# Decoder layer with 32 experts: the product of gate and up stays in SBUF on its way to the down product

## The chip, the cores and the metric

The kernel runs on one core of a Trainium2 chip. The core has a matrix engine (PE, with a separate stream for weight loads, PEld), a vector engine (DVE), a scalar engine (ACT), a general engine (POOL) and an engine that mostly issues transfers (SP). SP, ACT and POOL each have a queue from which they start transfers; all transfers run on the same 16 DMA engines. Every engine works through its own list in order and waits for others by semaphores. Matrix products accumulate in PSUM, everything else lies in SBUF (128 partitions) or in device memory (HBM).

The metric is the device time of the launch in microseconds. Before the change it was 3912.97 us, the median of three runs from 3909.75 to 3914.64.

## What is computed

One decoder layer in float32 on 32 sequences of 128 tokens of width 512: causal self-attention, cross-attention, and a mixture of experts with a shared expert. The change is in the experts. Each of 4096 tokens picks 6 of 32 experts; cut to what matters:

```python
g = ragged_dot(xs, w_gate, group_sizes)      # xs: tokens sorted by expert, width 512 -> 352
u = ragged_dot(xs, w_up, group_sizes)
d = ragged_dot(silu(g) * u, w_down, group_sizes)   # 352 -> 512
expert_out = sum over the 6 picks of d * weight
out = x + expert_out + shared(x)
```

## The kernel before

Self-attention and cross-attention fill the first half of the time. While cross-attention ends, tokens are routed: tables in memory say which token stands in which slot of which expert. The slots are cut into 208 tiles of 128 tokens, each of one expert. Four sets of weight buffers (`SETS`) are used in turn, and consecutive tiles belong to four different experts, so a set keeps its expert for several tiles; a register (`fresh`) says whether a weight transfer really has to be made, and a transfer that need not be made is skipped (`cond=new`).

`Experts.run` (from L1508) writes the order of PE, DVE, ACT and POOL out by hand. Iteration i does:

- `gate_up(i)`: PE multiplies the turned tokens `e_xT` with `wg` and `wu` (16 matmul records of 352 columns, L1447) into the two halves of a PSUM tile; ACT makes silu of the first half (`e_act`, L1451); DVE multiplies it with the second half (`e_gu`, L1452). `e_gu` is one buffer of 128 slots x 384 columns, of which 352 are written and the rest is zero. A transfer of ACT's queue writes it to memory (`e_gu_d`, L1454), cut into 4 runs of 96 columns.
- `turn_in(i + 2)`: DVE transposes gathered tokens in 32x32 blocks (`e_xr` to `e_xT`, L1434).
- `turn_out(i - 1)`: DVE transposes `e_gr` to `e_guT` in two instructions, 96 and 32 partitions (L1473).
- `weights_in(i + 4)`: SP's queue loads `wg` and `wu` (L1396) for the tile four on.
- `down(i - 2)`: PE multiplies `e_guT` with `wd` (6 matmul records of 512 columns, L1483); ACT scales by the routing weight (`e_y`, L1487); POOL's queue adds the rows into `sum_d` in memory (indirect, L1488). `weights_out(i + 2)` loads `wd` in two parts (L1408, L1411).
- `part_out(i)`: a second transfer of ACT's queue reads `e_gu_d` back as `e_gr` (L1463), so that partition 32q + s holds run q of the slots 4s to 4s + 3. It can be issued when the first has landed.
- `tokens(i + 5)`: four indirect gathers of POOL's queue (`e_xr`, L1422).

So the product of tile i has one iteration to become `e_gr`, and the transpose of it one more until PE needs it. PSUM has four tiles, taken in turn by `gate_up` and `down`. `e_y` and `e_gr` have two buffers each.

Before and after the experts stand groups of the shared expert (`Shared.group`, L1201 to L1262): three before, five after. Their work space (`s_p`), and that of cross-attention (`x_p2`), stay allocated during the experts. After `experts.run()` a conditional block handles more than 208 tiles; it is not entered here. The last groups end the kernel.

Of the kernel before, what the change touches and what calls it, by code (L numbers as in the profile page):

```python
# [10 lines left out]
F32 = mybir.dt.float32  # L11
# [7 lines left out]
P = 128  # L19
E = 512  # L20
# [1244 lines left out]
class Experts:  # L1265
# [14 lines left out]
    def __init__(  # L1280
        self, cm, ctx, table_ds, h3_d, sum_d, w_gate, w_up, w_down, eid, fresh, rows, n_tiles
    ):
        self.cm, self.h3_d, self.sum_d, self.eid, self.fresh = cm, h3_d, sum_d, eid, fresh
        self.w_in, self.w_out, self.n_tiles = (w_gate, w_up), w_down, n_tiles
        nc, tc = cm.nc, cm.tc

        def pool(name, bufs):
            return ctx.enter_context(
                tc.tile_pool(name=name, bufs=bufs, side="right", reuse_waits="tile")
            )  # L1290

        cp, self.p2 = pool("e_c", 1), pool("e_p2", 2)
        self.dram = ctx.enter_context(tc.tile_pool(name="e_dram", bufs=4, space=DRAM))
        T = h3_d.shape[0]
        self.T, self.cp, self.rows, self.table_ds = T, cp, rows, table_ds
        self.NT = rows.shape[1]
        self.wg = [cp.tile([P, EC, M], F32, name=f"wg{s}") for s in range(SETS)]
        self.wu = [cp.tile([P, EC, M], F32, name=f"wu{s}") for s in range(SETS)]
        self.wd = [cp.tile([P, len(M_CHUNKS), E], F32, name=f"wd{s}") for s in range(SETS)]

        self.gu_s = cp.tile([P, self.Q * self.RUN], F32, name="e_gu")

        self.row_i = cp.tile([P, 2], I32, name="e_row_i")
        self.row = cp.tile([P, 2], F32, name="e_row")
        self.last, self.expert = None, {}
        self.got, self.spread = {}, {}
        self.xr, self.xT, self.gu, self.gr, self.guT = {}, {}, {}, {}, {}

    def fetch(self):

        nc = self.cm.nc
        for j in range(self.NT):
            self.got[j] = [
                self.p2.tile([P, E], F32, name=("e_y", "e_xT")[j % 2])[:, 0 : 2 * P].rearrange(
                    "p (s o) -> p s o", o=2
                )
                for i in range(len(self.table_ds))
            ]
            for t, table_d in zip(self.got[j], self.table_ds):
                nc.gpsimd.indirect_dma_start(  # L1320
                    out=t.rearrange("p s o -> p (s o)"),
                    out_offset=None,
                    in_=table_d.rearrange("(n s) o -> n (s o)", s=P),
                    in_offset=bass.IndirectOffsetOnAxis(ap=self.rows[:, j : j + 1], axis=0),
                    bounds_check=table_d.shape[0] // P - 1,
                )
        nc.gpsimd.memset(self.gu_s, 0.0)
        nc.gpsimd.iota(self.row_i, pattern=[[0, 2]], base=self.T + 1, channel_multiplier=1)

    def arrange(self, j):  # L1330
# [108 lines left out]
    def gate_up(self, i):  # L1439
        if i >= self.end:  # L1440
            return
        nc = self.cm.nc
        pgu = self.cm.banks()
        t, s = self.xT.pop(i), i % SETS
        for half, w in enumerate((self.wg[s], self.wu[s])):
            for c in range(EC):
                nc.tensor.matmul(  # L1447
                    pgu[:, half, 0:M], t[:, c, :], w[:, c, :], start=c == 0, stop=c == EC - 1
                )
        act = self.p2.tile([P, M], F32, name="e_act", bufs=1)  # L1450
        nc.scalar.activation(act, pgu[:, 0, 0:M], AF.Silu)  # L1451
        nc.vector.tensor_tensor(self.gu_s[:, 0:M], act, pgu[:, 1, 0:M], ALU.mult)  # L1452
        self.gu[i] = self.dram.tile([self.Q, P, self.RUN], F32, name="e_gu_d")
        nc.scalar.dma_start(  # L1454
            out=self.gu[i].rearrange("q s m -> s q m"),
            in_=self.gu_s.rearrange("s (q m) -> s q m", q=self.Q),
        )

    def part_out(self, i):


        gr = self.gr[i] = self.p2.tile([P, self.Q, self.RUN], F32, name="e_gr")
        self.cm.nc.scalar.dma_start(  # L1463
            out=gr.rearrange("p t m -> p (t m)"),
            in_=self.gu.pop(i).rearrange("q (i t) m -> (q i) (t m)", t=self.Q),
        )

    def turn_out(self, i):
        g = self.gr.pop(i)
# [8 lines left out]
    def down(self, i):  # L1478
        nc = self.cm.nc
        py = self.cm.banks()[:, 0, :]  # L1480
        t, s = self.guT.pop(i), i % SETS
        for c, (_, n) in enumerate(M_CHUNKS):
            nc.tensor.matmul(  # L1483
                py, t[:n, c, :], self.wd[s][:n, c, :], start=c == 0, stop=c == len(M_CHUNKS) - 1
            )
        y = self.p2.tile([P, E], F32, name="e_y")
        nc.scalar.mul(y, py, self.weight[:, i : i + 1])  # L1487
        nc.gpsimd.indirect_dma_start(  # L1488
            out=self.sum_d[:, :],
            out_offset=bass.IndirectOffsetOnAxis(ap=self.into[:, i : i + 1], axis=0),  # L1490
            in_=y[:, :],
            in_offset=None,
            bounds_check=self.T + P - 1,
            compute_op=ALU.add,
        )
# [12 lines left out]
    def run(self):  # L1508


        first, en = self.first, mybir.EngineType
        with self.cm.tc.manual_schedule(engines={en.PE, en.DVE, en.Activation, en.Pool}):
            for i in range(first, first + 2):
                self.turn_in(i)
                self.tokens(i + 3)
            for i in range(first, self.end + 2):
                self.gate_up(i)
                self.turn_in(i + 2)
                if first < i <= self.end:
                    self.turn_out(i - 1)  # L1520
                self.weights_in(i + SETS)
                if i > first + 1:
                    self.down(i - 2)
                    self.weights_out(i - 2 + SETS)
                if i < self.end:
                    self.part_out(i)
                self.tokens(i + 5)


# [1 line left out]
def decoder_kernel(  # L1531
# [31 lines left out]
    with tc.tile_pool(name="x_w", bufs=1, side="right") as x_w:  # L1563
# [29 lines left out]
        s_w = SharedWeights(cm, s_w_pool, sw_gate, sw_up, sw_down)  # L1593
        s_h_pool = ctx.enter_context(tc.tile_pool(name="s_h", bufs=2, reuse_waits="tile"))
        shared = Shared(cm, s_h_pool, h3T_d, sum_d, out)
        p2 = ctx.enter_context(tc.tile_pool(name="x_p2", bufs=2, reuse_waits="tile"))
        cross.run(p2)
        x_ctx.close()
        s_pool = ctx.enter_context(tc.tile_pool(name="s_p", bufs=1, reuse_waits="tile"))
        shared.use(s_pool, s_w)  # L1600
        en = mybir.EngineType
        in_order = {en.PE, en.DVE, en.Activation, en.Pool}
# [19 lines left out]
    with tc.manual_schedule(engines=in_order):  # L1622
# [16 lines left out]
        shared.group(EARLY - 1, False, between)  # L1639
        while todo:  # L1640
            between()
    experts.run()
    many = nc.values_load(used[0:1, 0:1], min_val=1, max_val=n_tiles)
    with tc.If(many > usual):
        experts.begin(usual, n_tiles)
        experts.first_tokens()
        experts.run()
    done = EARLY * Shared.G
    for i in range(2):
        b = done // 2  # L1650
# [59 lines left out]
```

## Time and profile before

| | us |
|---|---|
| median of 3 runs | 3912.97 |
| profiled execution, device time | 3913.15 |
| its span, first to last instruction | 3911.4 |
| experts, first gate matmul to first matmul of the next shared group | 2024.05 to 3618.70 |
| PE busy in 2400 to 2800 us | 388.15 of 400 |
| DVE, ACT, POOL busy there | 135.89, 60.35, 299.81 |
| mean share of the 16 DMA engines there | 0.69 |
| issue of `e_gu_d`, of `e_gr` on ACT's queue | 0.366, 0.338 |

The profile is of one execution. A page gives busy times, slices and costly groups; a row of a group reads: line, engine, operation, out<-in, shapes, count, then busy time and mean ns of one, then the idle time of the engine just before such instructions and what ended most of it. A row of the timeline reads: start, duration, engine, line, operation, out<-in, shapes, count, and in brackets the engine's idle time before it with its releaser. A row of the waits reads: who waited for whom, total us, times, longest. "issue" and "remote" mean that the profile does not name a releaser. Matmul ends are modelled and overlap the next start a little.

### The profile page before, as it was taken

What the parts mean: (1) busy time and instruction counts of PE and PEld (TensorE: products, weight loads), DVE (VectorE), ACT (ScalarE), POOL (GpSimd) and SP (SyncE); (2) the same over time, 40 slices, a digit from 0 to 9 for tenths busy, and PEclk for the clock granted to TensorE, in tenths of its full rate; (3) what the DMA queues carried; (4) which work ended last, traced back from release to release, by engine and by line L of the source; (5) the groups of instructions that cost most, each with busy time, mean ns of one, the idle gap of its engine ahead of it and who ended that gap; (6) DMA issues with size and microseconds to landing.
All of it is one profiled execution on the core that took longest, in us unless ns stands there. A gap on an engine that the chain in (4) does not pass through costs nothing. (4 is left out here: it accounts for less than half of the span.)

```text
span 3911.4 us, 58185 instructions
## 1 busy us (share of the span) xinstructions
PE 3793.0 (97%) x19060; PEld 2015.6 (52%) x19060; DVE 2057.6 (53%) x3202; ACT 1678.9 (43%) x4032; POOL 2349.5 (60%) x2582
## 2 busy tenths in 40 slices
PE   8999999899999999999999999999999999999999
PEld 5666666434444444444445555555555555555444
DVE  5888888777877877776133333333333333332111
ACT  6989999757766776666101111111111111111000
POOL 3545545636777777775347777777777777775000
PEclk9999999899999999999999999999999999999999
DMA  3111110121111111111167777767667676766210
GB/s 110 34 34 38 37 34 27 43 87 57 53 60 47 47 47 47 49 47 50 52 178 168 164 166 170 174 151 174 160 153 167 161 170 147 181 151 150 80 64 32
DMA packets 285987, 387.21 MB, mean 99 GB/s; under 512 B 147888, under 2 KB 179248, under 8 KB 285616
## 3 DMA queue, kind: packets, MB, share of 16 engines
q0 software_dynamic: 62912, 109.85, 15.7%
q1 hardware_dynamic: 81792, 190.98, 15.4%
q10 hardware_dynamic: 140976, 82.60, 7.5%
q8 instruction: 154, 2.52, 0.3%
q14 instruction: 153, 1.25, 0.1%
HBM read 617.52 MB, written 143.07 MB: 194 GB/s over the span
## 5 line engine op out<-in xcount | busy, mean ns | idle before, releaser
L1422 POOL DMA_INDIRECT e_xr<-h_d,e_run_of x832 | 849.2, 1021 | 282.1 <-issue 268.1
L695 DVE TENSOR_REDUCE nm<-ps 128x2 f32<-128x1024 f32 x512 | 611.2, 1216 | 112.1 <-PE ps L691 105.3
L1452 DVE TENSOR_TENSOR e_gu<-e_act,ps 128x352 f32<-128x352 f32 x208 | 108.4, 521 | 974.4 <-ACT e_act L1451 548.8
L718 ACT ACTIVATE xp<-ps 128x1024 f32<-128x1024 f32 x512 | 505.9, 1021 | 265.0 <-PE ps L691 200.9
L1483 PE MATMUL ps<-wd,e_guT 128*128 128x512 f32 (+1 forms) x1248 | 585.2, 605 | 34.6 <-ACT e_y L1487 15.7
L714 PE MATMUL ps<-xqn,xk 32*128 32x512 f32 x2048 | 527.1, 620 | 20.6 <-ACT xp L718 19.2
L1447 PE MATMUL ps<-wu,e_xT 128*128 128x352 f32 x1664 | 528.6, 461 | 7.4 <-DMA wu<-in_L_ffn_w_up_dram 5.1
L1447 PE MATMUL ps<-wg,e_xT 128*128 128x352 f32 x1664 | 527.9, 460 | 5.3 <-DMA wg<-in_L_ffn_w_gate_dram 4.5
L691 PE MATMUL ps<-xk,xq 32*128 32x512 f32 x2048 | 526.9, 630 | 0.5 <-DVE nm L695 0.4
L1451 ACT ACTIVATE e_act<-ps 128x352 f32<-128x352 f32 x208 | 96.5, 464 | 935.2 <-PE ps L1447 443.7
L1488 POOL DMA_INDIRECT sum_d<-e_y,e_into x208 | 335.8, 1615 | 178.1 <-ACT e_y L1487 91.6
L1447 PEld LDWEIGHTS ps<-wg,e_xT 128*128 128x128 f32 x1664 | 315.1, 190 | 243.2 <-issue 108.8
L1447 PEld LDWEIGHTS ps<-wu,e_xT 128*128 128x128 f32 x1664 | 316.4, 191 | 186.6 <-DMA wu<-in_L_ffn_w_up_dram 8.3
L279 ACT ACTIVATE s<-s,a_nm 128x128 f32<-128x128 f32 x1024 | 395.7, 396 | 4.9 <-DVE a_nm L265 4.5
L1483 PEld LDWEIGHTS ps<-wd,e_guT 128*128 128x128 f32 (+1 forms) x1248 | 239.8, 194 | 291.7 <-issue 226.5
L1487 ACT ACTIVATE e_y<-ps,e_weight 128x512 f32<-128x512 f32 x208 | 143.0, 687 | 431.3 <-PE ps L1483 265.0
L714 PEld LDWEIGHTS ps<-xqn,xk 32*128 32x128 f32 x2048 | 168.6, 183 | 284.3 <-ACT xp L718 123.3
L1473 DVE STREAM_TRANSPOSE e_guT<-e_gr 96x384 f32<-96x384 f32 (+1 forms) x416 | 230.5, 554 | 76.2 <-DMA e_gr<-e_gu_d 53.5
L228 POOL TENSOR_SCALAR k<-kz,a_keep,a_extra 128x256 f32<-128x256 f32 x128 | 82.6, 655 | 287.4 <-ACT kz L227 287.4
L1028 POOL DMA_INDIRECT table_d<-entry,at x192 | 202.1, 1053 | 64.7 <-issue 53.2
L729 PE MATMUL ps<-xp,v 128*32 128x512 f32 x2048 | 233.0, 595 | 7.9 <-ACT xp L718 7.6
L1434 DVE STREAM_TRANSPOSE e_xT<-e_xr 128x512 f32<-128x512 f32 x208 | 226.3, 1088 | 8.8 <-DMA e_xr<-h_d,e_run_of 8.8
(272 smaller groups left out, 5282.6 us busy)
## 6 DMA issues: line engine op xcount, KB each, us to landing
wg<-in_L_ffn_w_gate_dram SPq DMA_DIRECT2D x208, 704.0 KB
wu<-in_L_ffn_w_up_dram SPq DMA_DIRECT2D x208, 704.0 KB
wd<-in_L_ffn_w_down_dram SPq DMA_DIRECT2D x208, 576.0 KB
e_gu_d<-e_gu ACTq DMA_DIRECT2D x208, 192.0 KB
e_gr<-e_gu_d ACTq DMA_DIRECT2D x208, 192.0 KB
wd<-in_L_ffn_w_down_dram SPq DMA_DIRECT2D x208, 128.0 KB
e_xr<-h_d,e_run_of POOLq DMA_INDIRECT x832
xres<-in_x_dram SPq DMA_DIRECT2D x32, 256.0 KB
```

What stands on the lines that cost most here:

```text
L279: nc.scalar.activation(s[:, j, c, side, :], s[:, j, c, side, :], AF.Exp, bias=nm[n][:, side, at : at + 1], accum_out=sm[n][:, to : to + 1],)
L691: self.nc.tensor.matmul(sc[:, i, :], q[rows, ts(c, P)], k[rows, :], start=True, stop=True)
L695: self.nc.vector.tensor_reduce(at[:, self.ROW[side], 2 * pair : 2 * pair + 2], sc, AX.X, ALU.max, negate=True)
L714: self.nc.tensor.matmul(sc[:, i, :], k[rows, ts(c, P)], q[rows, :], start=True, stop=True)
L718: self.nc.scalar.activation(e, sc, AF.Exp)
L729: self.nc.tensor.matmul(po[b, side][ts(j, 32), :], self.v2[b % 2][:, c, 2 * j + side, :], es[j // 2][:, j % 2, :], start=c == 0, stop=c == ...
L1422: self.cm.nc.gpsimd.indirect_dma_start(out=xr[:, t, :], out_offset=None, in_=self.h3_d.rearrange("t (q f) -> (t q) f", q=self.Q), in_offse ...
L1434: self.cm.nc.vector.transpose(xT.rearrange("p c (t i) -> p c t i", t=self.Q), self.xr.pop(i).rearrange("p t (j c) -> p c t j", c=EC),)
L1447: nc.tensor.matmul(pgu[:, half, 0:M], t[:, c, :], w[:, c, :], start=c == 0, stop=c == EC - 1)
L1473: self.cm.nc.vector.transpose(t[rows, 0:n, :].rearrange("p c (t i) -> p c t i", t=self.Q), g[rows, :, 0 : 32 * n].rearrange("p t (j c) -> ...
L1483: nc.tensor.matmul(py, t[:n, c, :], self.wd[s][:n, c, :], start=c == 0, stop=c == len(M_CHUNKS) - 1)
L1488: nc.gpsimd.indirect_dma_start(out=self.sum_d[:, :], out_offset=bass.IndirectOffsetOnAxis(ap=self.into[:, i : i + 1], axis=0), in_=y[:, :] ...
```

## The change

The memory tile `e_gu_d` and `part_out` go. After the multiplication, four transfers of ACT's queue each copy one run of 96 columns from all 128 partitions of `e_gu` to 32 partitions of `e_gr`, within SBUF. `e_gu` has two buffers instead of one, `e_gr` three instead of two, and the scaled output (`e_y`, now `e_out`) four instead of two. They lie in a new pool, opened in the space of `x_p2` and `s_p`, which are closed before the experts; after them the new pool is closed and `s_p` is opened again for the last shared groups.

```diff
-        nc.vector.tensor_tensor(self.gu_s[:, 0:M], act, pgu[:, 1, 0:M], ALU.mult)
-        self.gu[i] = self.dram.tile([self.Q, P, self.RUN], F32, name="e_gu_d")
-        nc.scalar.dma_start(
-            out=self.gu[i].rearrange("q s m -> s q m"),
-            in_=self.gu_s.rearrange("s (q m) -> s q m", q=self.Q),
-        )
-
-    def part_out(self, i):
-        gr = self.gr[i] = self.p2.tile([P, self.Q, self.RUN], F32, name="e_gr")
-        self.cm.nc.scalar.dma_start(
-            out=gr.rearrange("p t m -> p (t m)"),
-            in_=self.gu.pop(i).rearrange("q (i t) m -> (q i) (t m)", t=self.Q),
-        )
+        gu = self.gu_s[i % 2]
+        nc.vector.tensor_tensor(gu[:, 0:M], act, pgu[:, 1, 0:M], ALU.mult)
+        gr = self.gr[i] = self.p3.tile([P, self.Q, self.RUN], F32, name="e_gr", bufs=3)
+        for q in range(self.Q):
+            nc.scalar.dma_start(
+                out=gr[ts(q, 32)], in_=gu[:, ts(q, self.RUN)]
+            )
+
+    def room(self, pool):
+        self.p3 = pool
+        self.gu_s = [pool.tile([P, self.Q * self.RUN], F32, name=f"e_gu{i}") for i in range(2)]
+        for t in self.gu_s:
+            self.cm.nc.gpsimd.memset(t, 0.0)
...
-        y = self.p2.tile([P, E], F32, name="e_y")
+        y = self.p3.tile([P, E], F32, name="e_out", bufs=4)
...
-                if i < self.end:
-                    self.part_out(i)
...
+    x_out.close()
+    e_out = ExitStack()
+    experts.room(e_out.enter_context(tc.tile_pool(name="e_p3", bufs=1, reuse_waits="tile")))
     experts.run()
...
+    e_out.close()
+    shared.use(ctx.enter_context(tc.tile_pool(name="s_p", bufs=1, reuse_waits="tile")), s_w)
```

## The prediction

> **What bounds the kernel.** I read the busy times first, then the groups of PE in the experts, then the waits, then the timeline of one tile that goes well and one that doesn't.
>
> ```profile
> PE 3793.0 (97%) x19060; PEld 2015.6 (52%) x19060; DVE 2057.6 (53%) x3202; ACT 1678.9 (43%) x4032; POOL 2349.5 (60%) x2582
> L1483 PE MATMUL ps<-wd,e_guT 128*128 128x512 f32 (+1 forms) x1248 | 585.2, 605 | 34.6 <-ACT e_y L1487 15.7
> L1447 PE MATMUL ps<-wu,e_xT 128*128 128x352 f32 x1664 | 528.6, 461 | 7.4 <-DMA wu<-in_L_ffn_w_up_dram 5.1
> L1447 PE MATMUL ps<-wg,e_xT 128*128 128x352 f32 x1664 | 527.9, 460 | 5.3 <-DMA wg<-in_L_ffn_w_gate_dram 4.5
> ```
>
> PE is busy 97% of the span. In the experts it stands still for 34.6 + 7.4 + 5.3 = 47.3 us, no more; the change can win only there, and in what such pauses bring with them.
>
> ```profile
> 3590.84 2.74 PE L1483 MATMUL ps<-wd,e_guT 128*128 128x512 f32 x6
> 3591.10 0.46 ACT L1451 ACTIVATE e_act<-ps 128x352 f32<-128x352 f32 x1 [4.11 <-PE ps L1447]
> 3592.15 0.37 ACTq L1454 DMA_DIRECT2D e_gu_d<-e_gu  x1
> 3593.42 2.53 PE L1447 MATMUL ps<-wg,e_xT 128*128 128x352 f32 x8
> 3593.62 0.69 ACT L1487 ACTIVATE e_y<-ps,e_weight 128x512 f32<-128x512 f32 x1 [2.05 <-PE ps L1483]
> 3594.33 0.34 ACTq L1463 DMA_DIRECT2D e_gr<-e_gu_d  x1
> 3598.15 2.31 PE L1483 MATMUL ps<-wd,e_guT 128*128 128x512 f32 x5
> ```
>
> This is a good tile: silu starts 0.26 us after PE turned to the down product, and the next down product follows 7.31 us after the last. The first gate matmuls start at 2024.05 in the first tile and 3600.73 in the last: 207 distances, 1576.7 us. At 7.31 they would take 1513.2, so 63.5 us are lost: 47.3 (2.0 of it behind the last tile) by pauses, about 16 by the slow clock after them (PEclk is 0.86 in 3278 to 3290 us and 0.80 in 3564 to 3578, each with one pause, against 1.00; such stretches last 3 us, once 7).
>
> ```profile
> 3188.41 2.74 PE L1483 MATMUL ps<-wd,e_guT 128*128 128x512 f32 x6
> 3195.81 0.46 ACT L1451 ACTIVATE e_act<-ps 128x352 f32<-128x352 f32 x1 [10.85 <-remote]
> 3196.31 0.52 DVE L1452 TENSOR_TENSOR e_gu<-e_act,ps 128x352 f32<-128x352 f32 x1 [10.49 <-ACT e_act L1451]
> 3196.75 1.07 DVE L1434 STREAM_TRANSPOSE e_xT<-e_xr 128x512 f32<-128x512 f32 x1
> 3197.74 1.10 DVE L1473 STREAM_TRANSPOSE e_guT<-e_gr 96x384 f32<-96x384 f32 x2
> 3198.95 4.14 PE L1483 MATMUL ps<-wd,e_guT 128*128 128x512 f32 x6 [3.06 <-ACT e_y L1487]
> ```
>
> A bad tile: silu comes 7.40 us after PE turned to the down product. DVE multiplies, turns the tokens, and only then turns the product that PE needs. PE pauses 3.06 us. So silu may be 7.40 - 3.06 = 4.34 us late, and every us more is a pause. The releaser that the row names is not the cause; the order on DVE is.
>
> ```profile
> PE ps L1483 <- ACT e_y L1487: 15.7, 7, 3.1
> PE ps L1483 <- issue: 6.6, 6, 2.0
> PE ps L1483 <- DVE e_guT L1473: 6.3, 2, 4.1
> PE ps L1483 <- DMA wd<-in_L_ffn_w_down_dram: 5.9, 3, 2.2
> q10 hardware_dynamic: 140976, 82.60, 7.5%
> ```
>
> Down products that pause without waiting for `wd`: 15.7 + 6.6 + 6.3 = 28.6, less the 2.0 at the very end: 26.6 us. Weights: 47.3 - 2.0 - 26.6 = 18.7. Going through the 26.6 in the timeline, ten pauses (1.35, 1.78, 1.06, 2.42, 2.53, 2.93, 3.06, 1.66, 2.23, 4.09: 23.1 us) follow an idle ACT with nothing in its own queue to explain it, as at 3195.81, where the row says "remote"; four (1.74, 0.49, 0.99, 0.30: 3.5 us) follow an ACT that was held until `e_gu_d` had landed. The last fence's queue, q10, is ACT's.
>
> **The change, part by part.** *The hold on ACT.* The second transfer waits on ACT's queue until the first has landed, with the next silu behind it: 2.18 us from issue to issue in the good tile (3592.15 to 3594.33), 4.60 at 2608.54 to 2613.14. Silu waits for it, DVE for silu, PE for DVE. This wait goes: -3.5 us, the four pauses; at least 0, if the unexplained idleness takes its place, and no more, as the ten are not of it.
>
> *Four issues for two.* An issue takes 0.366 and 0.338 us; four at most 4 x (0.37 + 0.04) = 1.64. They start 1.05 us after silu (3591.10 to 3592.15) and end at 2.69; the scaling of y, 2.52 us after silu now, starts 0.2 us later and ends at 3.4 of 7.31. Next late is POOL's scatter: per tile POOL needs 4 x (1.02 + 0.30) + 1.62 + 0.30 = 7.2 us. Behind it wait only gathers for tiles three on. Cost 0; without the 3.9 us that ACT has left, 0.94 us per tile, 196 in all. In the built program each transfer of SP's and ACT's queues takes one of eight semaphores in turn and waits until the last user has landed. Six per tile made ACT's wait for a weight transfer of SP now and then, and SP's for ACT's; eight per tile make each wait for its own counterpart one tile earlier, 7.31 us ago. Taken as 0.
>
> *The way of the data.* No row shows a copy within SBUF. From below: the store lands within 2.18 us, and the new transfer is one such hop. From above: four one after another, 8.7 us. The product of the tile issued at 2608.54 is turned at 2616.75: 8.2 us. At the upper end DVE is 0.5 us late, within the 4.34. I take the lower, as they are issued without waiting for each other: 0. The Trainium skill, page "DMA: Bandwidth & Descriptors", "Rules for kernel authors", speaks against this part: transfers to disjoint partition parts share the same 16 engines and serialize, so one transfer of 128 partitions is better. No run here shows it yet; by it the sum is the same, as even the serial case fits.
>
> *Less traffic.* The stage moves 163 GB/s over 1594 us, 260 MB; a round trip of 2 x 192 KB x 208 = 82 MB (82.60 in the row) becomes 41 MB, 16% of all bytes less. Packets: q10 has 140976 in 7.5% of 16 x 3911 us, 33 ns each. After it 208 x 512 = 106496 stay: 73 us less per DMA engine at 33 ns, 4.6 points of the stage's 0.69. At the far end, the gather queue's 156 ns (62912 packets in 15.7%), they would add 745 us per engine; packets of 384 bytes are nearest to q10's own. The idleness of the ten is unexplained, so its price is bounded: 0 if the traffic has no part in it, -23.1 if all. I scale lateness with the bytes: pause = 0.84 x (pause + 4.34) - 4.34, which gives 0.44, 0.80, 0.20, 1.34, 1.43, 1.77, 1.88, 0.70, 1.18, 2.74, together 12.5: -11. Weights: 1.44 MB take 5.0 to 8.6 us to arrive; 16% less is about 1.1 us at each of 13 pauses, at most -12; since a PE that pauses less also asks earlier, -5, from 0 to -12.
>
> *Clock.* Nine stretches at half speed, about 1.7 us each: those behind pauses over 1.9. Four of the ten fall under that, and the longest gets shorter: -8; 0 to -16.
>
> *Buffers and space.* More buffers of y remove 13.5 us of POOL and a little of ACT, neither on PE's path: 0. Two fills of 0.44 us on POOL instead of one are placed among the routing, beside idle stretches of 12.57 and 14.85 us: 0. At the end the reopened space waits for the last scatter (issued 3620.39, 1.55 us). Silu of the shared group stands at 3625.87, and PE can fill four PSUM tiles of 6.86 us first: 27 us of cover: 0; without it, about 3.
>
> Sum: -3.5 - 11 - 5 - 8 = -27.5 against the profiled execution's 3913.15 (its span is 3911.4, 1.75 lie around it, and it is within 0.2 of the median): **3886**.
>
> **Rivals.** *The late signals stay.* PE's pauses come from what the trace doesn't name, and weights hide what is left: -3.5 with 0 to -4 by weights: 3906 to 3913. For it: the ten pauses have no cause in ACT's queue. Against: ACT's longest idles all stand directly behind the transfer that reads memory.
>
> *More landings, more late silu.* The mechanism: ACT gets late behind its transfers' completions; a tile now completes 4 + 5 of ACT and POOL instead of 2 + 5. Place: silu, L1451; it decides beyond 4.34 us. Lateness x 9/7: 1.286 x (23.1 + 43.4) - 43.4 = 42.1, +19 us, and as much clock as 19/47 of 16, +6: 3938. For it: the idle stands behind transfer issues. Against: nothing is late for want of ACT's time, 60 us busy in 400.
>
> *All pauses go.* The experts at 7.31 per tile: 3913 - 63.5 = 3850; POOL's 7.2 is next. Against: weights arrive at the DMA's pace. That the transfers aren't four, or go through memory, is ruled out by the built program, which lists four to `e_gr` per tile.
>
> **How the numbers follow.** Forecast (3868 to 3905) 0.47; all or nearly all pauses gone (3848 to 3868) 0.12; late signals stay (3905 to 3921) 0.21; more late silu (above 3921) 0.20. A measurement of this kernel can tell about 0.2%, 7.8 us. Faster is the first two and a small part of the third, 0.60; same 0.20; slower 0.20. The range from 3855 to 3922 leaves out most of the slow rival and the end of the best case, together some 0.2.
>
> **What would show it.** After: no row of `e_gu_d`; q10 with about 107,000 packets and 41 MB; L1483's idle near 15 to 18 us and not 34.6; L1447's together near 8; silu never held behind its queue. Right in mechanism if the down products pause less and silu is less often late; wrong if L1483's idle stays at 30 or grows, or if DVE waits for `e_gr`. A different stage's time would show a cost that I placed at 0.

## The result, and the profile after

The changed kernel was slower. It took 3944.98 us (median of 4 runs, 3941.12 to 3951.21) against 3911.36 (4 runs, 3909.07 to 3914.64) of the kernel before; the ratio is 1.0087, 95% interval 1.0069 to 1.0104. The forecast was 3886, range 3855 to 3922.

The busy times, the queue of ACT and the groups of PE in the experts, from the page of the changed kernel (span 3944.9 us):

```profile
PE 3798.7 (96%) x19060; PEld 2016.3 (51%) x19060; DVE 2052.9 (52%) x3202; ACT 1674.5 (42%) x4032; POOL 2349.6 (60%) x2583
q10 hardware_dynamic: 121008, 41.73, 4.3%
L1478 PE MATMUL ps<-wd,e_guT 128*128 128x512 f32 (+1 forms) x1248 | 592.5, 612 | 74.2 <-issue 73.8
L1443 PE MATMUL ps<-wg,e_xT 128*128 128x352 f32 x1664 | 527.2, 459 | 0.0
L1443 PE MATMUL ps<-wu,e_xT 128*128 128x352 f32 x1664 | 526.2, 459 | 0.0
```

The bytes went as planned (41.73 MB in ACT's queue, half of 82.60). The packets did not: ACT's queue has 121008 and not about 107,000, because each transfer also has 16 packets of 4 bytes (in the experts 208 x (512 + 4 x 16) = 119808), which the prediction left out. PE no longer stands still for gate and up weights at all (7.4 + 5.3 us before). But the pauses ahead of the down product grew from 34.6 to 74.2 us: +27 us of pauses in all. The distances between the first gate products of the 208 tiles now lose 98.9 us against 7.31 per tile, where it was 63.5. Of these 35 us more, 28 are pauses (73.5 instead of 45.3, without those behind the last tile) and the rest, 7, is the slow clock that follows them (11 half-speed stretches instead of nine). The other stages did not move: the next shared group starts 33.5 us later, all of it gathered in the experts.

The timeline of the worst pause shows how it comes (start, duration, engine, line; in brackets the idle time before):

```profile
2548.43 2.81 PE L1478 MATMUL ps<-wd,e_guT 128*128 128x512 f32 x6
2551.08 2.53 PE L1443 MATMUL ps<-wg,e_xT 128*128 128x352 f32 x8
2553.45 2.53 PE L1443 MATMUL ps<-wu,e_xT 128*128 128x352 f32 x8
...
2559.63 0.07 SPq L1392 DMA_DIRECT2D wu<-in_L_ffn_w_up_dram  x1
2559.70 0.46 ACT L1447 ACTIVATE e_act<-ps 128x352 f32<-128x352 f32 x1 [8.00 <-remote]
2560.19 0.52 DVE L1449 TENSOR_TENSOR e_gu<-e_act,ps 128x352 f32<-128x352 f32 x1 [11.87 <-issue]
...
2560.63 1.08 DVE L1430 STREAM_TRANSPOSE e_xT<-e_xr 128x512 f32<-128x512 f32 x1
2560.75 2.52 ACTq L1452 DMA_DIRECT2D e_gr<-e_gu  x4
2561.62 1.11 DVE L1468 STREAM_TRANSPOSE e_guT<-e_gr 96x384 f32<-96x384 f32 x2
...
2562.84 3.36 PE L1478 MATMUL ps<-wd,e_guT 128*128 128x512 f32 x4 [6.86 <-issue]
```

The up product that silu (2559.70) reads had ended by 2548.31, just before PE turned to the down product; silu comes 11.4 us later, and ACT had nothing else to do for 8.00 of them. SP's `wu` transfer, which waits for the same signal of PE, starts at the same instant, 2559.63. So it isn't ACT that is late, but PE's signal: the semaphore records have it at 2559.61. Signals between ACT and DVE were prompt: in every tile the multiplication starts 0.03 us after silu's end or after DVE's instruction before it. PE meanwhile ran on to 2555.97 and then stopped for 6.86 us, since the product of the tile before stands behind silu's multiplication on DVE. The pause is the lateness less 4.5, as the prediction's threshold of 4.34 says. It is the bad tile of before; there are now more of them. Of the 40 pauses ahead of down products (without the end), 37, with 71.6 of 73.5 us, follow a silu that is over 4 us late. Silu starts over 0.3 us late in 116 tiles instead of 91, and 441 us late in sum instead of 230.

Where a wait is named can mislead here: the waits put 320 us of idle time ahead of the scaling of y down to the landing of `e_gr`, but the built program has that instruction wait only for PE and for an old scatter.

What changed for SP can be read in its waits (queue, line, what for: us in total, times, longest us), first of the kernel before, then of the changed one, both from 2100 to 3500 us:

```profile
SPq L1411 <- DMA wd<-in_L_ffn_w_down_dram: 188.5, 52, 9.6
SPq L1411 <- DMA e_gr<-e_gu_d: 69.6, 21, 6.2
```

```profile
SPq L1404 <- remote: 76.3, 29, 5.1
SPq L1392 <- PE ps L1443: 75.6, 61, 2.9
SPq L1404 <- PE ps L1478: 73.4, 42, 5.5
```

Before, SP waited for other transfers (the semaphore of the `wd` transfer at L1411 was last used by another kind of transfer) and issued the `wu` load a median of 20.2 us after the PE signal that frees its buffer. In the changed kernel it waits for PE and issues 2.6 us after. That is why the weights are on time now.

### The profile page after: what moved, and what is told of

It reads as the page before. It is cut to its first block, busy times and chain, and to the rows that moved or that the text cites. A ratio compares the mean times of both kernels' runs of the same rounds, so it can differ in the third digit from the quotient of the medians.

```text
span 3944.9 us, 58820 instructions
## 1 busy us (share of the span) xinstructions
PE 3798.7 (96%) x19060; PEld 2016.3 (51%) x19060; DVE 2052.9 (52%) x3202; ACT 1674.5 (42%) x4032; POOL 2349.6 (60%) x2583
## 3 DMA queue, kind: packets, MB, share of 16 engines
q10 hardware_dynamic: 121008, 41.73, 4.3%
q8 instruction: 154, 2.52, 0.3%
## 5 line engine op out<-in xcount | busy, mean ns | idle before, releaser
L1478 PE MATMUL ps<-wd,e_guT 128*128 128x512 f32 (+1 forms) x1248 | 592.5, 612 | 74.2 <-issue 73.8
L1483 POOL DMA_INDIRECT sum_d<-e_out,e_into x208 | 335.8, 1615 | 214.9 <-ACT e_out L1482 106.1
L1482 ACT ACTIVATE e_out<-ps,e_weight 128x512 f32<-128x512 f32 x208 | 142.9, 687 | 747.7 <-DMA e_gr<-e_gu 329.5
```

Of the source, the lines that this page charges most:

```text
L1478: nc.tensor.matmul(py, t[:n, c, :], self.wd[s][:n, c, :], start=c == 0, stop=c == len(M_CHUNKS) - 1)
L1483: nc.gpsimd.indirect_dma_start(out=self.sum_d[:, :], out_offset=bass.IndirectOffsetOnAxis(ap=self.into[:, i : i + 1], axis=0), in_=y[:, :] ...
```

## The experiments

Eighteen runs were made in six series (the expectations say "call"), each series on one chip with the kernel before beside it. The table gathers what the traces of those with late signals say, without e7_order and e8_order_mem, which have a limit of their own. "SP behind" is the median from the end of PE's up products to SP's issue of the `wu` load that waits for them. "Silu late" is the sum over the tiles of silu's start after the end of the up products, where over 0.3 us, from the third tile on. Pauses are PE's, over 0.1 us, in the experts, ahead of the down product and ahead of the gate and up products. Transfers are those of SP and ACT per tile. Ratios are to the kernel before in the same series. Each trace is of one execution: in e10_older and e11_seven the executions spread over 28 us, and the traced one was the fastest (3931.81) and the slowest (3958.98) of four.

| kernel | transfers | SP behind | silu late | pauses down | gate, up | ratio (95%) |
|---|---|---|---|---|---|---|
| before | 6 | 20.2 | 230 | 34.5 | 12.7 | 1 |
| e1_buffers | 6 | 20.3 | 257 | 35.1 | 10.4 | 0.9995 (0.9985 to 1.0004) |
| e3_two | 6 | 20.7 | 270 | 40.2 | 15.4 | 1.0020 (1.0008 to 1.0032) |
| e11_seven | 7 | 22.5 | 184 | 29.2 | 47.5 | 1.0082 (1.0052 to 1.0111) |
| after | 8 | 2.6 | 441 | 74.2 | 0.0 | 1.0087 (1.0069 to 1.0104) |
| e2_transfers | 8 | 2.6 | 482 | 89.6 | 0.0 | 1.0126 (1.0108 to 1.0144) |
| e5_small_act | 8 | 1.2 | 496 | 74.2 | 0.0 | 1.0093 (1.0064 to 1.0122) |
| e6_small_sp | 8 | 1.6 | 396 | 62.8 | 2.8 | 1.0085 (1.0059 to 1.0112) |
| e10_older | 8 | 8.7 | 380 | 59.5 | 1.7 | 1.0111 (1.0085 to 1.0136) |
| e12_turn_in | 8 | 3.0 | 507 | 72.4 | 0.1 | 1.0086 (1.0064 to 1.0109) |
| e9_deep | 8 | 7.4 | 994 | 9.1 | 39.2 | 1.0061 (1.0042 to 1.0081) |
| e4_load4 | 9 | 22.8 | 178 | 13.9 | 70.8 | 1.0172 (1.0154 to 1.0190) |

### First series: which part of the change costs

**e1_buffers.** The new buffers in the reopened space, with the round trip through memory.

```diff
+        nc.scalar.dma_start(
+            out=self.gu[i].rearrange("q s m -> s q m"),
+            in_=gu.rearrange("s (q m) -> s q m", q=self.Q),
+        )
...
-        for q in range(self.Q):
-            nc.scalar.dma_start(
-                out=gr[ts(q, 32)], in_=gu[:, ts(q, self.RUN)]
-            )
+        self.cm.nc.scalar.dma_start(
+            out=gr.rearrange("p t m -> p (t m)"),
+            in_=self.gu.pop(i).rearrange("q (i t) m -> (q i) (t m)", t=self.Q),
+        )
```

> The round trip through memory is kept (one store, one load per tile on ACT's queue); only the buffers of the change are taken over (two e_gu, three e_gr, four of y, in the reopened space). Theory 'count': the loss comes from more transfers per tile on ACT's queue, each with an issue and a landing, which make PE's completion signals reach ACT late; the buffers have no part: 3905 to 3915 us, idle before the down product near 35 us. Rival 'buffers': the new buffers or their place cost it: 3935 to 3950 us.

3907.03 us against 3908.80. The buffers and their place cost nothing, and by themselves bring nothing.

**e2_transfers.** The four transfers with the old numbers of buffers.

```diff
-        gu = self.gu_s[i % 2]
+        gu = self.gu_s[0]
...
-        gr = self.gr[i] = self.p3.tile([P, self.Q, self.RUN], F32, name="e_gr", bufs=3)
+        gr = self.gr[i] = self.p3.tile([P, self.Q, self.RUN], F32, name="e_gr", bufs=2)
...
-        y = self.p3.tile([P, E], F32, name="e_out", bufs=4)
+        y = self.p3.tile([P, E], F32, name="e_out", bufs=2)
```

> The changed kernel with the old numbers of buffers (one e_gu, two e_gr, two of y); the four transfers within SBUF stay. Theory 'count': 3938 to 3955 us, down product idle 70 us or more. Rival 'buffers': 3900 to 3915 us. If the extra buffers helped, above 3955 us.

3960.46 us: the loss belongs to the transfers, and the extra buffers seem to hide about 0.4% of it (1.0126 here, 1.0087 for the whole change, from two series). That is above the expected upper end of 3955: with silu late, buffers seem to matter.

**e3_two.** Two of the four transfers; the quarters that are not copied stay zero.

```diff
-        for q in range(self.Q):
+        for q in (0, 3):
```

> The changed kernel with two of the four transfers per tile (the first and the last quarter; the two middle quarters of the product are left out and read as zeros). Theory 'count': two issues and two landings per tile on ACT as before the change, so the lateness goes back at least to that of before: 3885 to 3915 us, down product idle under 40 us. Rival 'path': the copy from SBUF to SBUF is what disturbs, half of it is left: 3920 to 3935 us.

3916.69 us. Six transfers per tile again, SP 20.7 us behind again, and nearly the time of before, though the copy is within SBUF and moves a quarter of the bytes of before (21.26 MB in ACT's queue). It is 1.7 us above the range of 'count' and slower than before by a little (1.0020, 1.0008 to 1.0032): with the fewest bytes of all these kernels, silu was later than before (270 us).

**e4_load4.** The kernel before with its load cut into four.

```diff
-        self.cm.nc.scalar.dma_start(
-            out=gr.rearrange("p t m -> p (t m)"),
-            in_=self.gu.pop(i).rearrange("q (i t) m -> (q i) (t m)", t=self.Q),
-        )
+        src = self.gu.pop(i).rearrange("q (i t) m -> (q i) (t m)", t=self.Q)
+        for q in range(self.Q):
+            self.cm.nc.scalar.dma_start(
+                out=gr[ts(q, 32)].rearrange("p t m -> p (t m)"), in_=src[ts(q, 32)]
+            )
```

> The kernel before, its one load per tile cut into four loads of 32 partitions each, in the same place on ACT's queue; the same bytes and the same way through memory, five transfers per tile on ACT instead of two. Theory 'count': slower than before by at least what the change cost, 3935 to 3970 us, with silu more often late. Rival 'path': 3905 to 3920 us, as nothing moves within SBUF.

3973.20 us, in the range of 'count', but not for its reason. The groups of PE from its page:

```profile
L1484 PE MATMUL ps<-wd,e_guT 128*128 128x512 f32 (+1 forms) x1248 | 576.7, 598 | 13.9 <-issue 4.3
L1447 PE MATMUL ps<-wg,e_xT 128*128 128x352 f32 x1664 | 543.4, 470 | 38.3 <-DMA wg<-in_L_ffn_w_gate_dram 21.0
L1447 PE MATMUL ps<-wu,e_xT 128*128 128x352 f32 x1664 | 533.7, 464 | 32.5 <-DMA wu<-in_L_ffn_w_up_dram 28.5
```

The down product hardly pauses; the weights are late. With nine transfers per tile over eight semaphores SP waits for ACT's transfers: at L1396, between 2100 and 3500 us, 170.8 us for `e_gu_d` and 115.8 for `e_gr`, against 3.2 in the kernel before. Silu is late by 178 us only. So 'count' as I had written it, more landings make later signals, fell here: the most transfers gave the least lateness.

### Second series: the number alone, and another order

**e5_small_act, e6_small_sp.** The kernel before plus two transfers of 16 bytes per partition that nothing reads, issued by ACT or by SP.

```diff
+    def extra(self, i, queue):
+        for k in range(2):
+            queue.dma_start(out=self.small[1 + 2 * (i % 3) + k], in_=self.small[0])
```

> The kernel before, unchanged, with two more transfers per tile on ACT's queue that copy 16 bytes per partition within SBUF and that nothing reads: as many transfers per tile as in the changed kernel (eight on the queues of SP and ACT), but the product goes through memory in one store and one load. Theory 'count': the number of transfers per tile is what makes PE's signals late: 3930 to 3955 us, down product idle 60 us or more. Weights should then be on time as in the changed kernel, as each transfer again shares its semaphore with its own counterpart of the tile before: first products idle under 3 us. Rival 'path': the copy of the product within SBUF does it: 3895 to 3915 us.

> As the run with two small transfers on ACT's queue, but both are issued by SP, behind the gate and up weights. Theory 'count': no matter who issues, 3930 to 3955 us. Rival 'issue': it is the time or the place of issue on ACT's queue that makes silu late: 3895 to 3915 us here, and slow only with the small transfers on ACT. Rival 'path': 3895 to 3915 us in both.

3945.85 and 3939.52 us. The page of the first:

```profile
L1490 PE MATMUL ps<-wd,e_guT 128*128 128x512 f32 (+1 forms) x1248 | 593.7, 613 | 74.3 <-issue 47.9
L1450 PE MATMUL ps<-wg,e_xT 128*128 128x352 f32 x1664 | 527.4, 459 | 0.0
L1450 PE MATMUL ps<-wu,e_xT 128*128 128x352 f32 x1664 | 526.2, 459 | 0.0
```

These are the pauses of the changed kernel, 74.3 and 0 and 0, with the product still going through memory. So neither the product's way within SBUF nor the bytes nor the issuing engine makes the loss. The two small transfers copy within SBUF too, but e3_two, with two such copies and six transfers, lost only 0.2%. Eight transfers per tile make it, and what comes with eight in these traces is that SP is on time. That the pauses hang on silu holds here for the greater part: 58.6 of 72.2 us follow a silu over 4 us late.

**e7_order, e8_order_mem.** On DVE the turns stand ahead of the multiplication, in the changed kernel and in e1_buffers. `gate_up` ends with silu there, and `product` holds the multiplication and the transfers (in e8_order_mem the store); the turned tiles have three buffers each.

```diff
                 self.gate_up(i)
-                self.turn_in(i + 2)
                 if first < i <= self.end:
                     self.turn_out(i - 1)
+                self.turn_in(i + 2)
+                self.product(i)
```

> The changed kernel with another order on DVE: the turn of the last tile's product and the turn of the tokens stand ahead of the multiplication that waits for silu, instead of behind it; three buffers of e_xT and e_guT in the reopened space make that possible. If the pauses come from silu being late by more than 4.3 us, as all theories here have it, silu may now be about 8 us late before PE pauses: down product idle under 25 us, 3875 to 3905 us. Rival: PE waits for the landing of the transfers and not for what stands behind silu; then the order does nothing: 3935 to 3955 us.

> The same new order on DVE with the round trip through memory kept (and the new buffers). Lateness of silu as before the change, allowance about 8 us: the down product's pauses shrink from 35 to under 10 us, those for weights stay or grow: 3875 to 3900 us. If the load of the product lands too late for the earlier turn, DVE's multiplication waits behind it and the gain is lost: 3905 to 3930 us.

3997.94 us (1.0248, 1.0208 to 1.0288) and 4170.28 us (1.0675, 1.0647 to 1.0704): both far off. The timeline of e7_order in a good tile says why:

```profile
2600.85 0.48 DVE L1456 TENSOR_TENSOR e_gu<-e_act,ps 128x352 f32<-128x352 f32 x1
...
2601.37 2.51 ACTq L1459 DMA_DIRECT2D e_gr<-e_gu  x4
...
2605.28 1.17 DVE L1475 STREAM_TRANSPOSE e_guT<-e_gr 96x384 f32<-96x384 f32 x2 [3.94 <-DMA e_gr<-e_gu]
...
2606.47 1.10 DVE L1430 STREAM_TRANSPOSE e_xq<-e_xr 128x512 f32<-128x512 f32 x1
2607.50 0.48 DVE L1456 TENSOR_TENSOR e_gu<-e_act,ps 128x352 f32<-128x352 f32 x1
```

Multiplication, issue, landing, turn, turn, next multiplication: a loop of 6.65 us (2607.50 - 2600.85) that I had made myself, against 7.31 per tile. Whatever is late once can hardly be caught up. With the way through memory the loop has a second hop in it; the tiles of e8_order_mem follow each other at 8.83 us on average. The run also gives the landing that the prediction had only bounds for: the turn starts 3.9 us after the first of four issues, 1.4 after the end of the last.

### Third series: more allowance, an older signal, seven transfers

**e9_deep.** The order of e7_order with the down product one tile later, so that the loop has two tiles; `e_gr` has four buffers. Against e7_order, the main lines are:

```diff
-                    self.turn_out(i - 1)
+                    self.turn_out(i - 2)
...
-                    self.down(i - 2)
-                    self.weights_out(i - 2 + SETS)
+                    self.down(i - 3)
+                    self.weights_out(i - 3 + SETS)
```

> The changed kernel with the down product one tile later (three tiles behind the gate products instead of two): on DVE the turn of the product of two tiles ago and the turn of the tokens stand ahead of the multiplication that waits for silu. The loop from the multiplication through issue, landing and turn to the next multiplication, about 7 us, now has two tiles of 7.31 us to go round in; in the earlier run with the new order it had one, and no slack. Silu may be some 8 us late (then the PSUM tile of its products is missed). Theory 'late silu': down product idle under 15 us, 3855 to 3885 us. Rival: PE pauses for something that doesn't hang on silu: 3920 to 3955 us.

3930.26 us; neither theory had it. The groups:

```profile
L1485 PE MATMUL ps<-wd,e_guT 128*128 128x512 f32 (+1 forms) x1248 | 577.2, 595 | 9.4 <-issue 6.5
L1443 PE MATMUL ps<-wg,e_xq 128*128 128x352 f32 x1664 | 538.3, 464 | 25.1 <-issue 17.2
L1443 PE MATMUL ps<-wu,e_xq 128*128 128x352 f32 x1664 | 535.1, 460 | 14.4 <-issue 14.2
```

The down product is free, as expected, but silu got later, 994 us in sum, until PE stopped at the gate and up products instead. The trace names a releaser for 7.7 of these 39 us only: DVE's multiplication, which reads the PSUM tile that PE wants next. It looks as if the allowance grew and the lateness filled it; why silu is later here than in the other kernels of the table is not shown.

**e12_turn_in.** Only the turn of the tokens ahead of the multiplication, which stands in `product` again.

```diff
                 self.gate_up(i)
                 self.turn_in(i + 2)
+                self.product(i)
                 if first < i <= self.end:
                     self.turn_out(i - 1)
```

> The changed kernel with the turn of the tokens ahead of the multiplication on DVE and the turn of the product still behind it (three buffers of e_xT). The way from silu to the down product gets shorter by one turn of 1.07 us, so silu may be 5.4 us late and not 4.3: each of some 40 pauses gets shorter by up to 1.07 us. Theory 'late silu': down product idle 40 to 55 us, 3915 to 3932 us. Rival: pauses don't hang on DVE's order: 3938 to 3955 us.

3944.32 us, 72.4 us of pauses as without it; silu's lateness went from 441 to 507 us. Again the larger allowance seems to have been filled, and the expected 25 us didn't come.

**e10_older.** SP asks for gate and up weights one tile later.

```diff
-                self.weights_in(i + SETS)
+                if i > first:
+                    self.weights_in(i + SETS - 1)
```

> The changed kernel; SP asks for the gate and up weights of a tile one tile later, so that its transfer waits for a PE signal that is already a tile old, and no more for the very signal that silu waits for. Theory 'SP beside silu': the signals are late because SP, since it is no longer held back by ACT's transfers, comes to its wait at the same moment as ACT: down product idle back under 45 us, 3885 to 3920 us. Rival 'count': eight transfers per tile make the signals late wherever SP waits: 3935 to 3955 us.

3948.19 us, as 'count' had it. That SP waits for the same signal as silu is not the reason.

**e11_seven.** e5_small_act with one small transfer instead of two.

```diff
-        for k in range(2):
+        for k in range(1):
```

> The kernel before with one small transfer within SBUF more on ACT's queue: seven transfers per tile on the queues of SP and ACT. Theory 'count': between six (3907) and eight (3946): 3918 to 3932 us, down product idle 45 to 60 us, whether weights are late or not. Rival 'alignment': only at eight does each transfer share its semaphore with its own counterpart; at seven SP still waits for ACT's transfers and stays some 20 us behind, down product idle 25 to 40 us: 3900 to 3918 us, unless the weights come later still.

3945.47 us, above both ranges. As 'alignment' had it, SP stays 22.5 us behind and the down product pauses 29.2 us; what rose is the weights, 47.5 us. Of the three numbers tried at which the semaphores rotate between the queues (six, seven, nine), six is the mildest.

### What the lateness goes with

In three traces silu is on time, or less late, soon after a stop of PE and gets later as PE runs on, up to some 30 us. The table gives the mean time that silu starts after both the up products' end and ACT's previous instruction, by the time since the last stop of PE of over 0.4 us (the first and last tiles left out):

| since the stop, us | to 7.5 | to 15 | to 22.5 | to 30 | to 37.5 | more |
|---|---|---|---|---|---|---|
| before | 0.10 | 0.28 | 0.48 | 0.63 | 1.35 | 1.09 |
| after | none | 0.68 | 1.49 | 1.90 | 1.60 | 1.76 |
| e9_deep | 0.02 | 0.16 | 1.82 | 4.59 | 2.46 | 2.52 |

In the worst pause of the changed kernel, PE's products end at 2551.24, 2553.61 and 2555.97 and their three signals come at 2562.49, 2562.58 and 2562.67, when PE has long stopped. A stop for weights thus also lets the signals catch up. This would explain why fewer stops for weights brought more of the other kind, and it is what the next series was to test. But the stops can't be all of it: at the same time since a stop, silu is later in the changed kernel than before in every column that has tiles of both.

### Fourth to sixth series: stops on purpose, and chips without late signals

**e13_pause3, e14_pause6, e15_deep_pause4.** A small matmul that reads silu's result makes PE stop in every third or sixth tile of the changed kernel, or in every fourth of e9_deep.

```diff
+        at, act = self.act
+        if at == i + 2 and at % 3 == 0:
+            nc.tensor.matmul(both[0:32, 1, 0:64], act[:, 0:32], act[:, 0:64], start=True, stop=True)
         t, s = self.guT.pop(i), i % SETS
```

> The changed kernel with one deliberate short stop of PE in every third tile: a matmul of 32 x 64 that reads silu's result of the same tile stands ahead of the down product, so PE waits there until silu has run, about 0.7 us if the signal is on time. Nothing reads what it writes. Transfers stay four per tile. Theory 'pause clears': PE's signals fall behind only while PE runs without a stop, and a stop clears them; 69 stops of 0.7 to 1.0 us (48 to 69 us) take the place of the 74 us of pauses: silu's lateness summed over the tiles falls from 441 us to under 200, the down product itself pauses under 20 us, 3915 to 3945 us. Rival 'count': the lateness comes from eight transfers per tile and stays; the stops come on top, and each lasts as long as silu is late: 3985 to 4050 us.

> The same with a stop in every sixth tile (35 stops, 25 to 35 us if silu is on time). Theory 'pause clears': lateness between the two, since it is near 0 for two tiles after a stop and grows after that: 250 to 400 us in sum, 3925 to 3955 us. Rival 'count': 3965 to 4000 us.

> The kernel with the down product one tile later, and a stop in every fourth tile (52 stops of some 0.7 us, 36 us). Theory 'pause clears': lateness under 300 us in sum instead of 994, no more pauses of PE beside the stops than 15 us: 3885 to 3910 us, at or below the kernel before. Rival 'count': the stops come on top of 3930: 3965 us and more.

3922.80, 3882.46 and 3902.54 us, silu on time in every tile but one or two. But the kernel before, without any stop, ran beside them in 3853.85 us, where it had taken 3906 to 3911 in every series until then. So these runs show the price of a stop, 1.11 us per stopped tile (8.42 us instead of 7.31), and not whether it clears anything.

**e16_after, e17_pause3.** The changed kernel and e13_pause3 again, on the next chip.

> The changed kernel itself, again, on the chip that this call is given. In the last call the kernel before took 3853.9 us and silu was on time in all tiles of the three kernels with stops, so either the stops or that chip keep the signals on time. If this call's kernel before is near 3854 too: theory 'the chip makes the signals late': 3838 to 3850 us, faster than before by the 10 us of its pauses for weights (3922.8 less 69 stops of 1.11 us is 3846; 3882.5 less 35 is 3844). Rival 'only stops clear': 3880 us or more, with silu late. If this call's kernel before is near 3908: 3938 to 3952 us, as measured first.

> The changed kernel with a stop in every third tile, again. If this call's kernel before is near 3908 (late signals): theory 'the chip makes the signals late, stops don't clear them': silu late by 200 us or more in sum, 3960 to 4010 us. Rival 'a stop clears': under 100 us, 3918 to 3930 us. If this call's kernel before is near 3854: 3918 to 3927 us as in the last call, which tells nothing new.

The kernel before took 3852.57 us here too, the changed kernel 3852.98 (10 runs, ratio 1.0003, 0.9993 to 1.0013), e17_pause3 3919.66. Without stops silu was on time. So on such a chip the change makes no difference that can be measured. My 3838 to 3850 was too low: it left out pauses that this kernel has (12.4 us, below) and the kernels with stops have not, perhaps because a stop also gives POOL time.

**e18_before.** The kernel before for its trace.

> The kernel before the change, itself, for its trace on the chip that this call is given. If it runs near 3853 us: silu on time in nearly all tiles, SP still some 20 us behind, and pauses of PE for weights and gathers together near the 12 us that the changed kernel has there, which would show why the change is worth nothing where signals are on time. Rival: pauses for weights near 10 us and no others, so that the changed kernel's 12.4 us are of its own making. If it runs near 3908 us: silu late by 200 to 260 us in sum and 45 to 50 us of pauses, a second sample of what the first trace shows.

3852.06 us. The groups of PE in its page, and then in that of e16_after (whose profiled execution was its slowest, 3860.72):

```profile
L1483 PE MATMUL ps<-wd,e_guT 128*128 128x512 f32 (+1 forms) x1248 | 570.0, 593 | 2.0 <-issue 2.0
L1447 PE MATMUL ps<-wg,e_xT 128*128 128x352 f32 x1664 | 528.1, 460 | 4.7 <-DMA wg<-in_L_ffn_w_gate_dram 4.7
L1447 PE MATMUL ps<-wu,e_xT 128*128 128x352 f32 x1664 | 527.1, 460 | 2.3 <-DMA wu<-in_L_ffn_w_up_dram 2.2
```

```profile
L1478 PE MATMUL ps<-wd,e_guT 128*128 128x512 f32 (+1 forms) x1248 | 573.6, 595 | 12.4 <-issue 9.3
L1443 PE MATMUL ps<-wg,e_xT 128*128 128x352 f32 x1664 | 526.3, 458 | 0.0
L1443 PE MATMUL ps<-wu,e_xT 128*128 128x352 f32 x1664 | 526.2, 459 | 0.0
```

Here the trade is seen without late signals, as far as one execution of each goes. The change removes 7.0 us of pauses for weights, as SP is on time (0.0 us behind instead of 17.7), and takes on seven pauses ahead of the down product. The timeline of e16_after shows the first:

```profile
2762.28 1.08 DVE L1430 STREAM_TRANSPOSE e_xT<-e_xr 128x512 f32<-128x512 f32 x1 [6.41 <-DMA e_xr<-h_d,e_run_of]
...
2763.29 1.11 DVE L1468 STREAM_TRANSPOSE e_guT<-e_gr 96x384 f32<-96x384 f32 x2
...
2764.49 2.81 PE L1478 MATMUL ps<-wd,e_guT 128*128 128x512 f32 x6 [2.43 <-issue]
```

DVE waits 6.41 us for gathered tokens, and the turn of the product stands behind. All seven have such a wait, of 4.1 to 6.7 us; in sum DVE's turn of the tokens is idle 225.3 us for them, against 8.3 in e18_before. POOL, which issues the gathers and needs 7.2 us per tile, is what the prediction named as the next bound once PE runs at 7.31. In e16_after its last gather issue for a tile ends a median of 3.8 us after the gate products of two tiles earlier begin, in e18_before 4.5 us before they begin; why POOL falls behind with the change is not shown. In e18_before silu starts 0.8 to 3.8 us late in ten tiles, each time directly behind the issue of the load of `e_gr` on ACT's queue. That is the hold on ACT; it stays under 4.34 us, and the down product pauses only at the end (2.0 us). On these chips 3850, the time of the rival "all pauses go", is where both kernels already are.

## Why the prediction was wrong

**The step that failed** is "I scale lateness with the bytes" under *Less traffic*, with -11 us of the sum. The bytes did fall as computed (258.14 to 217.20 MB in the experts), and the lateness nearly doubled, 230 to 441 us. e5_small_act has more bytes than before and the same pauses as the changed kernel; e3_two has the fewest and is no better than before. The lateness has nothing to do with this traffic that the runs could show. I had said that its cause was unknown and that 0 was the lower bound of the gain; this term had no loss in it, and that was the fault: a wait of unknown cause may grow as well as shrink. In place of a gain of 0 to 23.1 us, L1483's idle grew from 34.6 to 74.2 us, which the prediction had named as the sign of a wrong mechanism.

**The semaphores of the transfers**, "Taken as 0", were the second failed step, and they stand where the loss begins. I had seen that eight per tile make each transfer wait for its own counterpart, and had put no price on what SP does when it no longer waits for ACT's transfers. It went from 20.2 us behind to 2.6. Two transfers more per tile, with nothing else of the change, give the loss (e5_small_act, e6_small_sp). How they make PE's signals later stays open; that SP then waits for the same signal as silu is not the reason (e10_older).

**Weights**, -5 with bounds 0 to -12: the right sign, and larger, -12.7 at the gate and up products, but by SP's earlier issue and not by less traffic. e3_two, with the least traffic, still pauses 15.4 us for them.

**Clock**, -8: it followed the pauses the other way, about +7. The 1.9 us that the prediction reads as the limit is not exact: in the trace of before, pauses of 1.94, 2.52 and 2.53 us (at 2498, 2948 and 2936 us) have no slow stretch behind them. The clock's share there is 18 us and not 16, since 2.0 of the 47.3 us lie behind the last distance.

**The hold on ACT**, -3.5: `e_gu_d` is gone and nothing is held for its landing, but the gain can't be seen among 74 us of pauses; in e18_before the hold costs no pause. **Four issues** were mis-sized: 2.51 us in the row above and not 1.64. ACT has the time; e6_small_sp, where ACT issues two per tile, loses as much. **The way of the data** at a price of 0 was right: 3.9 us from the first issue to the turn in e7_order, between the bounds of 2.18 and 8.7. The rule of the Trainium skill that the prediction weighed against four transfers (page "DMA: Bandwidth & Descriptors", "Rules for kernel authors") told to use one transfer. Here the number did decide, but by what it did to the semaphores: the four had landed 1.4 us after the last issue, so serializing, if there was any, cost nothing that shows.

**Buffers, end**: 0 was right (e1_buffers 0.9995; the other stages unmoved).

**The rival "more landings, more late silu"** had the place, the threshold and nearly the time (3938), but not the mechanism: nine transfers gave the least lateness and the largest loss in the table, by late weights. That its number came near is luck.

What is shown: eight transfers per tile on the queues of SP and ACT give the loss of the change, whoever issues them, in the series with late signals (seven and nine lose too there, by late weights); in the one series without late signals in which the changed kernel ran, it lost nothing. That most of its pauses follow a late silu, and silu a late signal of PE, is read from the trace. What is only argued: that a stop of PE clears the signals, so that stops removed at one place return at another. The traces agree with it (the table by time since the stop; e9_deep and e12_turn_in, where lateness seems to have filled the allowance). But it isn't the whole of it, since at the same time since a stop silu is later in the changed kernel than before (from 0.68 against 0.28 us to 1.76 against 1.09). The run that was to settle it met a chip without late signals. No kernel here beats the kernel before; e1_buffers equals it.

## What to carry to other kernels

Where semaphores are handed out in turn, as here, adding or removing a transfer changes which transfers share one, and so how far ahead a queue that isn't touched can run: look in the built program at who waits for whose, on every queue, and price both sides. A wait whose cause the profile doesn't name may grow under a change as well as shrink, and a longer allowance may only be filled by more lateness. Before moving work ahead of a wait in an in-order list, add up the loop that it closes; and measure the kernel before on more than one chip, if a gain of one per cent is at stake.

## What the runs showed of the hardware that was not expected

- **PE's completion signals can arrive many microseconds late**, 11.3 us after the end of the products in the rows above (2548.31 to 2559.61), and then several within 0.1 us of each other. In the experts 40 such pairs under 0.15 us are in the first trace of before and 69 in that of after; in e18_before and e16_after there is none.
- **Semaphore updates are missing from the records in the same traces**, of transfers most of all. In the experts, before and after hold 455 and 487 of PE's 620 updates and 4396 and 4000 of the some 16300 by which POOL's transfers land; e18_before and e16_after hold 620 and 616, and 16276 and 16093. So sums of waits may not be comparable between the two kinds of trace. Whether the recording itself has a part in the late signals, no run here tells.
- **It depended on the chip, or on the time.** The kernel before took 3906 to 3911 us in the first four comparisons (one with the changed kernel, then three series on three chips), and 3853 to 3854 in the last three series, on three others. Which of the two it is wasn't tried.
- **SP goes slow beside it**: 222 and 224 of its register, check and wait instructions in the experts took 0.6 to 0.8 us in the first traces of before and after, none in e18_before and e16_after. Of these, 33 and 84 lie between the end of up products and a late silu, which is 14% and 27% of the time, so they don't gather there much, and one need not cause the other.
- The Trainium skill, page "Perfetto Trace Analysis", section "Tensor Engine Instruction (MATMUL, LD_WEIGHTS)", says that a matmul's end in the profile is an estimate and that its semaphore update is pushed after PSUM acknowledges the writes. That leaves room for a signal after the row's end; that it can be 11 us, this case shows (2548.31 to 2559.61).
- **An issue within SBUF takes longer**: 0.61 us median for each of four 32-partition transfers on ACT's queue, 0.37 for the store and the load through memory.
